# An empty step ahead of the deltas of a selective scan's chunk

## The chip, the cores and the metric

The kernel runs on one core of a Trainium2 chip. The time is device microseconds of one execution of the whole program; the number used is the median of several executions.

## What is computed

The reference takes eight images of 64 x 64 pixels with 96 channels through two layers. Only the first matters here. After a group norm, a projection and a 3 x 3 depthwise convolution, it runs a selective scan (the core of a state-space model) over the 4,096 pixels in four directions `k`, for 192 inner channels with 16 states each:

```python
dts   = einsum('bkrl,kdr->bkdl', x_dbl[:, :, :6], dt_proj_w)
delta = softplus(dts + dt_proj_b)
dA = exp(delta * A)
h  = dA * h + (delta * u) * B
y  = einsum('bkdn,bkn->bkd', h, C)
```

`x_dbl` holds, for each pixel, 6 numbers from which the deltas are made and 16 each of B and C; it is itself a product of the convolved pixels `u` with `x_proj_w`. The four directions are summed, normalised, gated, projected and added to the image. The second layer is a small perceptron on a spectrally upsampled image, filtered and sampled down again.

## The kernel before

**Chunks and tiles.** Each image and direction is cut into 4 chunks of 1,024 pixels, 128 chunks in all. A chunk has 24 tiles: a tile is 8 channels times 16 states on the 128 partitions, with the 1,024 pixels along the free dimension. So there are 3,072 tiles, and the main loop has a step for each. Step numbers below are counted from the chunk's first tile, 0 to 23; tile i is scanned in step i.

**What a tile needs.** TensorE spreads the deltas of 8 channels to 128 partitions with six matmuls into a PSUM tile `pd` (`decay`, L1087), and ScalarE takes the exponential in place (L1095). GpSimd multiplies the fetched delta times u, `dub`, by the broadcast B (`product_b`, L1080). VectorE scans (L1102). The product with C, `hc` (L1108), is made by VectorE for two tiles of three, and by GpSimd for the third (tile number 2 modulo 3), whose scan writes to its own tile `h` and not over `pd`. TensorE adds up the states (`sums`, L1141). `pd` has two buffers, so the decay of tile i + 1 waits until tile i - 1 is done with its buffer: after its scan where GpSimd makes the product, after VectorE's product elsewhere.

**The order of the work.** It is written out by hand; each engine takes its instructions in the order in which the program emits them. Step i issues, in this order: the fetch of tile i + 6 on SyncE's queue, GpSimd's product with C for tile i - 1 if it is GpSimd's, the product with B for tile i + 3, the decay and exponential of tile i + 1, the scan of tile i with VectorE's product and the copy of its last state, then `side.advance`, which lets the side work emit some pieces, and at every second step the sums.

**Side work.** Everything that is not a tile's own is a generator: the convolution, the gates, the perceptron, and `prepare` (L956), which makes what the chunk after needs. Each `yield` states the cost of the piece behind it on each engine and whether it needs one of three PSUM banks. `Side.advance` (L109) adds an allowance to each engine's budget at every step (CAPS, L50) and resumes the running generators, one piece each, if budget and banks allow; a piece marked `more` may follow in the same step, and a piece that doesn't fit waits for the next step. The preparation of a chunk is in the urgent list and goes ahead of the other work, after the stores. `Side.start` (L95) begins a new generator: it fetches the first yield and, if what that asks for is there, runs the first piece in the same step; up to two urgent items can begin in one step.

**The preparation of a chunk**, during the chunk before it. `begin` loads `u`. From step 0 on, `project` (L976) makes the product of `u` with `x_proj_w` in three pieces (L984, bank `px`), and after the third ScalarE copies it with a bias to `xd` (L994). `project` runs alone, so `broadcasts` (B and C to the partitions, by DMA from `xd`, L1005) and `deltas` (L1007) begin in the step in which it ends. `deltas` takes a bank `pv` and, for three groups of 64 channels: the product of `xd` with `dt_w` on TensorE (L1017); absolute value and exponential on ScalarE (L1026, L1027); a piece later logarithm and relu (L1029, L1030), which give softplus; their sum by a matmul with the identity (L1032), copied to `dl` and, as bfloat16, to `dp` (L1035, L1036); then two pieces that subtract what the bfloat16 copy holds and copy the rest (L1041, L1042), with GpSimd's product delta times u (L1040) and the DMAs that write it to memory (L1044). Each group takes five steps. The next group's product comes in the step after the last piece of the group before.

Of the kernel before, what the change touches and what calls it, by code (L numbers as in the profile page):

```python
# [137 lines left out]
def kernel(ctx: ExitStack, tc: tile.TileContext, a: dict, out: bass.AP):  # L138
# [817 lines left out]
    def prepare(b, k, i0, got):  # L956

        v = {}

        def begin():  # L960
            yield {}
            blocks = range(i0 // MB, i0 // MB + 2) if k % 2 else range(8)
            while not all((b, n, blk) in filtered for blk in blocks for n in range(2)):
                yield {}
            assert k % 2 or all((b, n) in laid for n in range(2))
            v["u"] = pp.tile([128, Q3, MB], F32, tag="u", name="u", bufs=1)
            for q in range(Q3):
                yield dict(dma=256)
                for hf in range(2):
                    t0 = i0 + MB * hf  # L970
                    nc.sync.dma_start(
                        v["u"][64 * hf : 64 * hf + 64, q, :], u_dram[b][k % 2][64 * q : 64 * q + 64, t0 : t0 + MB]
                    )
            got["du"] = dr.tile([DI, T], F32, tag="du", name="du")

        def project():  # L976

            xd = v["xd"] = pp.tile([128, MB], F32, tag="xd", name="xd", bufs=1)
            yield dict(bank=1, pe=0.95)
            n, p = side.bank("px")  # L980
            for q in range(Q3):
                for hf in range(2):
                    rows = slice(64 * hf, 64 * hf + 64)
                    nc.tensor.matmul(  # L984
                        p[rows],
                        xp[rows, k, q, :],
                        v["u"][rows, q, :],
                        start=(q == 0),
                        stop=(q == 2),
                        skip_group_check=True,  # L990
                    )
                if q < 2:
                    yield dict(pe=0.95, act=0.7 * q)
            nc.scalar.activation(xd, p, AF.Identity, bias=one)  # L994
            side.give(n)

        def broadcasts():

            xd = v["xd"]
            for name, row in (("br", 48), ("cr", 32)):  # L1000
                t = got[name] = pp.tile([128, T], F32, tag=name, name=name)
                for hf in range(2):
                    yield dict(dma=256)
                    src = xd[64 * hf + row : 64 * hf + row + NS, None, :]
                    nc.sync.dma_start(t[:, MB * hf : MB * hf + MB], src.to_broadcast([NS, 8, MB]))  # L1005

        def deltas():  # L1007

            yield dict(bank=1, pe=0.95, act=1.4)
            n, t = side.bank("pv")  # L1010
            for q in range(Q3):
                if q:
                    yield dict(pe=0.95, act=1.4)
                    t = side.again(n, "pv")
                for hf in range(2):
                    rows = slice(64 * hf, 64 * hf + 64)
                    nc.tensor.matmul(  # L1017
                        t[rows],
                        dt_w[rows, k, 64 * q : 64 * q + 64],
                        v["xd"][rows],  # L1020
                        start=True,
                        stop=True,
                        skip_group_check=True,
                    )
                e = pp.tile([128, MB], F32, tag="e", name="e")
                nc.scalar.activation(e, t, AF.Abs)  # L1026
                nc.scalar.activation(e, e, AF.Exp, scale=-1.0)  # L1027
                yield dict(act=1.4)
                nc.scalar.activation(e, e, AF.Ln, bias=1.0)  # L1029
                nc.scalar.activation(t, t, AF.Relu)  # L1030
                yield dict(pe=0.87, act=1.4)
                nc.tensor.matmul(t, ident, e, start=False, stop=True, skip_group_check=True)  # L1032
                dl = pp.tile([128, MB], F32, tag="e", name="dl")
                dp = got["dp", q] = pp.tile([128, 3, MB], BF16, tag="dp", name="dp", bufs=4)
                nc.scalar.copy(dl, t)  # L1035
                nc.scalar.copy(dp[:, 0, :], t)  # L1036
                for p in range(1, 3):
                    yield dict(pe=0.3, act=0.7, pool=1.3 * (p == 1))
                    if p == 1:
                        nc.gpsimd.tensor_tensor(v["u"][:, q, :], dl, v["u"][:, q, :], ALU.mult)  # L1040
                    nc.tensor.matmul(t, minus, dp[:, p - 1, :], start=False, stop=True, skip_group_check=True)  # L1041
                    nc.scalar.copy(dp[:, p, :], t)  # L1042
                for hf in range(2):
                    nc.sync.dma_start(  # L1044
                        got["du"][64 * q : 64 * q + 64, MB * hf : MB * hf + MB], v["u"][64 * hf : 64 * hf + 64, q, :]
                    )
                got["ready"] = q + 1
            side.give(n)

        return [(1, 0, begin), (1, 0, project), (4, 0, broadcasts), (4, 0, deltas)]  # L1050

    tiles = []
# [314 lines left out]
```

## Time and profile before

| | |
|---|---|
| median of 3 runs | 10,889.11 us (10,886.95 to 10,890.89) |
| the profiled execution, its own time | 10,889.88 us |
| its span, first to last instruction | 10,888.1 us |
| granted TensorE clock, mean | 0.977 |
| before the first scan | 139.2 us |
| between the starts of the first and the last scan | 10,471.3 us, 3,410 ns a step |
| after the start of the last scan | 277.7 us |
| busy: GpSimd (POOL), VectorE (DVE) | 10,172.5 us, 9,965.6 us |
| busy: TensorE (PE), ScalarE (ACT) | 9,406.6 us, 6,891.4 us |

In the profile's lines an engine is followed by the source line, the operation, the tile written and, after `<-`, those read. "idle before" is time in which that engine stood still ahead of those instructions, and the name behind it is what ended the wait. A line of the waits gives the total in microseconds, how often, and the longest.

### The profile page before, as it was taken

To read this page: it belongs to the slowest core of one execution; us is meant where nothing else is said; L and a number is where in the kernel's file an instruction comes from. 1 tells how busy PE (TensorE), PEld (TensorE's weight loads), DVE (VectorE), ACT (ScalarE), POOL (GpSimd) and SP (SyncE) were. 2 spreads that over 40 slices of the span, in tenths; PEclk is the share of its full clock that TensorE was granted. 3 is DMA by queue.
4 is the path that set the end of the run, shared out by engine and by line. 5 is a ranking of instruction groups with operands and counts; after the bars stand their busy time and mean duration, and the time that the engine had idled before them with its cause. 6 is when DMAs were issued, how large, how long until landed. Compare 5 with 4: busy or idle time off the path is not lost. (4 is left out here: it accounts for less than half of the span.)

```text
span 10888.1 us, 152912 instructions
## 1 busy us (share of the span) xinstructions
PE 9406.6 (86%) x52498; PEld 3129.1 (29%) x52498; DVE 9965.6 (92%) x7319; ACT 6891.4 (63%) x10138; POOL 10172.5 (93%) x4674
## 2 busy tenths in 40 slices
PE   7788778988789988899889997898978989789888
PEld 2222222422233222332223322233222432223325
DVE  5999999999999999999999999999999999999990
ACT  5666556767567665666656666566756767566653
POOL 4999999999999999999999999999999999999990
PEclk8999999999999999999999999999999999999998
DMA  6879898898988989898998989899898898988981
GB/s 155 224 200 234 218 236 216 221 235 232 239 214 225 235 233 233 214 225 232 240 228 220 230 223 247 217 225 234 231 237 218 222 232 234 239 214 223 230 207 49
DMA packets 1052725, 2402.30 MB, mean 221 GB/s; under 512 B 302012, under 2 KB 322748, under 8 KB 1051944
## 3 DMA queue, kind: packets, MB, share of 16 engines
q1 hardware_dynamic: 1050968, 2391.48, 87.0%
q8 instruction: 413, 6.77, 0.3%
q14 instruction: 368, 3.01, 0.1%
q10 hardware_dynamic: 976, 1.04, 0.0%
HBM read 1929.05 MB, written 328.73 MB: 207 GB/s over the span
## 5 line engine op out<-in xcount | busy, mean ns | idle before, releaser
L1080 POOL TENSOR_TENSOR bb<-dub,br 128x1024 f32<-128x1024 f32 x3072 | 7183.5, 2367 | 149.2 <-DMA dub<-du 95.6
L1095 ACT ACTIVATE pd<-pd,neg_a 128x1024 f32<-128x1024 f32 x3072 | 3339.4, 1087 | 3051.3 <-PE pd L1087 3026.1
L1102 DVE TENSOR_TENSOR_SCAN pd<-pd,carry,bb 128x1024 f32<-128x1024 f32 x1536 | 3605.4, 2347 | 279.3 <-ACT pd L1095 162.6
L1087 PE MATMUL pd<-dp,sel_b 64*128 64x512 bf16 x18432 | 2596.7, 385 | 1075.4 <-DVE carry L1122 686.6
L1108 DVE TENSOR_TENSOR hc<-pd,cr 128x1024 f32<-128x1024 f32 x2048 | 2508.7, 1225 | 144.8 <-PE py L1141 3.2
L1108 POOL TENSOR_TENSOR hc<-h,cr 128x1024 f32<-128x1024 f32 x1024 | 2423.0, 2366 | 180.3 <-DVE h L1102 151.4
L1102 DVE TENSOR_TENSOR_SCAN h<-pd,carry,bb 128x1024 f32<-128x1024 f32 x768 | 1797.5, 2341 | 1.7 <-ACT pd L1095 1.6
L1141 PE MATMUL py<-hc,sel_r 128*32 128x512 f32 x12288 | 1736.0, 620 | 48.6 <-POOL hc L1108 47.1
L1087 PEld LDWEIGHTS <-sel_b 64*128 64x128 bf16 x18432 | 722.7, 94 | 3602.7 <-issue 1557.1
L1102 DVE TENSOR_TENSOR_SCAN pd<-pd,bb 128x1024 f32<-128x1024 f32 x512 | 1173.3, 2292 | 128.2 <-ACT carry L1122 52.2
L565 PE MATMUL pc<-pad,convr 96*128 96x512 f32 (+1 forms) x2304 | 844.0, 610 | 2.1 <-issue 2.1
L1115 PE MATMUL idle<-xp,ident 128*128 128x384 f32 x1450 | 662.9, 540 | 3.2 <-ACT t1s L807 3.2
L1102 DVE TENSOR_TENSOR_SCAN h<-pd,bb 128x1024 f32<-128x1024 f32 x256 | 583.7, 2280 | 14.8 <-ACT pd L1095 11.6
L1040 POOL TENSOR_TENSOR u<-dl,u 128x512 f32<-128x512 f32 x384 | 491.7, 1280 | 108.7 <-ACT dl L1035 108.7
L1017 PE MATMUL pv<-xd,dt_w 64*64 64x512 f32 x1536 | 425.4, 632 | 166.9 <-ACT xd L994 164.5
L1141 PEld LDWEIGHTS py<-hc,sel_r 128*32 128x32 f32 x12288 | 253.4, 109 | 977.2 <-issue 751.4
L859 PEld LDWEIGHTS p<-w2q,mq 128*100 128x100 f32 x4800 | 461.9, 168 | 169.3 <-issue 135.2
L852 PE MATMUL ph<-xu,w 96*128 96x500 f32 x960 | 493.6, 617 | 16.0 <-ACT xu L846 9.2
L859 PE MATMUL p<-w2q,mq 128*100 128x96 f32 x4800 | 504.2, 256 | 2.3 <-ACT mq L853 2.3
L1032 PE MATMUL pv<-e,ident 128*128 128x512 f32 x768 | 437.1, 651 | 27.9 <-ACT pv L1030 27.0
L1042 ACT CAST dp<-pv 128x512 bf16<-128x512 f32 x768 | 452.1, 589 | 5.0 <-PE pv L1041 5.0
L984 PE MATMUL px<-u,xp 64*64 64x512 f32 x1536 | 417.2, 618 | 5.1 <-DMA u<-u 3.2
(162 smaller groups left out, 8195.4 us busy)
## 6 DMA issues: line engine op xcount, KB each, us to landing
dub<-du SPq DMA_DIRECT2D x3072, 512.0 KB
u<-u SPq DMA_DIRECT2D x768, 128.0 KB
du<-u SPq DMA_DIRECT2D x768, 128.0 KB
y<-yq SPq DMA_DIRECT2D x768, 128.0 KB
br<-xd SPq DMA_DIRECT2D x256, 256.0 KB
cr<-xd SPq DMA_DIRECT2D x256, 256.0 KB
yp<-y SPq DMA_DIRECT2D x384, 128.0 KB
yp<-u SPq DMA_DIRECT2D x192, 128.0 KB
```

Source lines behind the costliest of these rows:

```text
L565: nc.tensor.matmul(t[rows].rearrange("p (i j) -> p i j", i=8), weights[:, cs], v["pad"][:, 8 * blk + kw : 8 * blk + kw + 8, kh : kh + H], ...
L852: nc.tensor.matmul(t[:, :px], w1[:, m, :], xu, start=True, stop=True)
L859: nc.tensor.matmul(t[:SIDE, C * i : C * i + C], sq[:, m, row], w2q[:, m, :], start=(m == 0), stop=(m == 2))
L1040: nc.gpsimd.tensor_tensor(v["u"][:, q, :], dl, v["u"][:, q, :], ALU.mult)
L1042: nc.scalar.copy(dp[:, p, :], t)
L1080: nc.gpsimd.tensor_tensor(t["bb"], t["dub"], t["got"]["br"], ALU.mult)
L1087: nc.tensor.matmul(pd[:, MB * hf : MB * hf + MB], sel_b[rows, 4 * t["s"] + t["j"]].rearrange("p n c -> p (n c)"), t["got"]["dp", t["q"]][r ...
L1095: nc.scalar.activation(pd, pd, AF.Exp, scale=neg_a[:, t["k"], t["g"] : t["g"] + 1])
L1102: nc.vector.tensor_tensor_scan(t["h"][:, ::step], pd[:, ::step], t["bb"][:, ::step], 0.0 if t["first"] else held, ALU.mult, ALU.add)
L1108: (nc.gpsimd if t["by_pool"] else nc.vector).tensor_tensor(t["hc"], t["h"], t["got"]["cr"], ALU.mult)
L1115: nc.tensor.matmul(p, ident, xp[:, 0:2].rearrange("p k q r -> p (k q r)"), start=True, stop=True)
L1141: nc.tensor.matmul(py[r0 : r0 + 32], sel_r[:, t["j"], :], t["hc"][:, MB * hf : MB * hf + MB], start=(t["j"] == 0), stop=(t["j"] == 3 and t ...
```

## The change

One empty step is put at the head of the deltas' generator. An empty `yield {}` needs no budget and no bank: when `deltas` is begun, it runs up to the next yield, and what stands there, the first product of `xd` with `dt_w`, comes in a later step. Everything behind it in the generator moves along.

```diff
         def deltas():
 
+            yield {}
             yield dict(bank=1, pe=0.95, act=1.4)
             n, t = side.bank("pv")
             for q in range(Q3):
```

Lines from L1009 on stand one lower in the changed kernel.

## The prediction

> **What bounds the kernel now.** I read the page first: shares of the engines, then the costliest groups.
>
> ```profile
> PE 9406.6 (86%) x52498; PEld 3129.1 (29%) x52498; DVE 9965.6 (92%) x7319; ACT 6891.4 (63%) x10138; POOL 10172.5 (93%) x4674
> L1080 POOL TENSOR_TENSOR bb<-dub,br 128x1024 f32<-128x1024 f32 x3072 | 7183.5, 2367 | 149.2 <-DMA dub<-du 95.6
> L1102 DVE TENSOR_TENSOR_SCAN pd<-pd,carry,bb 128x1024 f32<-128x1024 f32 x1536 | 3605.4, 2347 | 279.3 <-ACT pd L1095 162.6
> ```
>
> POOL and DVE are both nearly full: three steps hold three scans and two products on DVE (3 x 2.35 + 2 x 1.23 = 9.5 us) and four products of 2.37 us on POOL (9.5 us). From the second to the second-last chunk POOL stands idle for 306 us, DVE for 536 us. No more than this idle time can be won, and only where DVE's wait makes POOL wait too. The waits say what ends them:
>
> ```profile
> DVE pd L1102 <- ACT pd L1095: 202.8, 246, 2.8
> ...
> PE pv L1017 <- ACT xd L994: 164.5, 107, 2.8
> ...
> ACT e L1026 <- PE pv L1017: 139.1, 113, 2.1
> ```
>
> Second line: in 107 places PE stands still at the first product of the deltas, because ScalarE has not copied `xd` yet. Third: ScalarE then waits for that product. First: DVE waits for exponentials. The timeline of one such place, steps 2 to 4 of the 36th chunk, ties the three together (start, duration, engine, line; idle before in brackets):
>
> ```profile
> 3003.37 0.82 PE L1087 MATMUL pd<-dp,sel_b 64*128 64x512 bf16 x6
> ...
> 3004.12 1.07 PE L984 MATMUL px<-u,xp 64*64 64x512 f32 x4
> ...
> 3004.23 1.09 ACT L1095 ACTIVATE pd<-pd,neg_a 128x1024 f32<-128x1024 f32 x1 [2.73 <-PE pd L1087]
> 3005.24 0.59 ACT L1174 COPY yq<-py 128x512 f32<-128x512 f32 x1
> ...
> 3005.72 0.70 ACT L994 ACTIVATE xd<-px,one 128x512 f32<-128x512 f32 x1
> ...
> 3006.47 1.08 PE L1017 MATMUL pv<-xd,dt_w 64*64 64x512 f32 x4 [1.27 <-ACT xd L994]
> ...
> 3007.48 0.82 PE L1087 MATMUL pd<-dp,sel_b 64*128 64x512 bf16 x6
> 3007.59 0.60 ACT L1026 ACTIVATE e<-pv 128x512 f32<-128x512 f32 x1 [1.17 <-PE pv L1017]
> ...
> 3008.22 0.63 ACT L1027 ACTIVATE e<-e 128x512 f32<-128x512 f32 x1
> ...
> 3008.76 1.07 ACT L1095 ACTIVATE pd<-pd,neg_a 128x1024 f32<-128x1024 f32 x1
> ...
> 3009.93 2.36 DVE L1102 TENSOR_TENSOR_SCAN pd<-pd,carry,bb 128x1024 f32<-128x1024 f32 x1 [0.89 <-ACT pd L1095]
> ```
>
> One step holds a chain over two engines: px, xd, pv, absolute value, exponential. Tile 4's decay and exponential are queued behind it, and scan 4 starts 0.89 us late.
>
> **How much room a step has.** Set the end of scan 2 at 0; the decay of tile 4 can start then. Scan 3 with its product ends at 3.6. An exponential starts 0.86 us after its decay's start and takes 1.09, so that of tile 4 must start by 2.5. That of tile 3 ends at about 0 (its decay could start when scan 2 did). ScalarE's side work of step 2 has thus some 2.5 us. It holds the copy of `yq` 0.59, `xd` 0.70, the wait 1.17, 0.60 and 0.63: 3.7, so 1.2 too much, against 0.89 measured here. In the same way the side work of a step 0 modulo 3 has some 3.8 us before a scan is late, and that of 1 modulo 3 some 2.5.
>
> **How often.** I laid the trace against the program's order. The first product stands in the same step as `xd` in 106 chunks: step 2 in 98, step 3 in 7, step 7 in the first. In those 98 DVE's idle time between the starts of scans 3 and 4 is 107.2 us, 1.09 each; in the other 30 chunks, where the product comes a step later (no bank was free) or both fall elsewhere, it is 0.05. The 7 lose 0.95 more than the others, a step later. The trace thus holds its own comparison.
>
> **The change, part by part.** The counts are from the program order of both kernels.
>
> *What goes.* After the change no chunk has `xd` and the first product in one step; 97 chunks have them in steps 2 and 3, 16 in 3 and 4, 14 in later pairs. 98 x (1.09 - 0.05) = 102 us, and 7 x 0.95 = 7. Sum 109.
>
> *What is late next.* Step 2 keeps `yq` and `xd` on ScalarE, 1.3 us of 2.5. Step 3 gets the product and 1.23 us of ScalarE work, of 3.8; the product runs while ScalarE is in tile 4's exponential.
>
> *What moves.* All five pieces of each group come a step later, so the products of the three groups go from residues 2, 1, 0 modulo 3 to 0, 2, 1. From the second chunk on, residues 0, 1, 2 hold 126, 132 and 120 of them after and 126 each before, with the wait for `xd` in 98 of residue 2 and 7 of residue 0. 28 products at residue 2 without the wait are in the trace: DVE's idle time in the step that follows is 0.17 each, no more than the 0.24 of all such steps. So the 92 more cost nothing by this row; if not, see the second rival. GpSimd's delta times u (1.28 us) keeps its count at about the same residues. The 768 DMAs that write it pass one more fetch of `dub` on SP's queue; the first is issued in step 7 and read from step 18 on, 11 steps or 37 us later, so this is covered. The broadcasts stay in the step of `xd`. The chunk's last pieces end at about step 18 instead of 17 of 24.
>
> *What is added.* Eight matmuls that keep TensorE busy in empty steps (725 to 733, each two rows of 0.54 us in the trace), 9 us in steps with almost nothing else on PE. All other work is the same by count. Ahead of the first scan the order changes too: ScalarE and the convolution in front of the first group's identity matmul keep the group's end near 112 us by the rows there; I take 0, within 2 either way. The work behind the last scan is the same.
>
> *What POOL takes back.* In 29 of the 98 chunks POOL's idle time is below the stall; together these stalls are 28 us. POOL runs ahead: its product ends in the median 5.3 us before the scan that reads it, at the least in those chunks 1.1 to 2.9, in three of them 0.3 to 0.8. That lead lets DVE gain one or two stalls before POOL ends last. Bounds 0 and 28; I take 12, nearer to 0, as most such chunks stand singly or in pairs.
>
> *The remaining idle time.* Only 602 of 3,064 steps keep the same list of side matmuls, so the 536 - 114 = 422 us of other idle time on DVE is dealt anew. I take 5 against the change, within 25 either way (6% of it, an estimate).
>
> Sum: -102 - 7 + 12 + 5 = -92. On the profiled execution, 10,889.9 - 92 = 10,798; the median of the runs lies 0.8 below that execution: **10,797**.
>
> **Two rules of the skill.** POOL has the highest share, 93% against DVE's 92%. The Trainium skill, Perfetto Trace Analysis, section Identifying the Most-Contended Engine, says to improve the engine with the highest occupancy first; this change takes nothing from POOL, and read strictly the rule leaves the first rival's time instead of the sum. Its section Optimization Strategy adds that a gap that repeats on the engine that should be full can mean too few buffers; the gap here repeats in 98 chunks and is 0.05 us in 30 with the same buffers, so the trace puts it to order, and by the rule the change would leave all 107 us in place.
>
> **Rivals.** *POOL sets the pace.* For: 97% of the window from 5,000 to 7,000 us:
>
> ```profile
> 5000.00:7000.00 2000.00, 1747.90 (x9576) 549.78 (x9576) 1895.47 (x1386) 1298.00 (x1899) 1936.92 (x888) 0.98 0.91 229
> ```
>
> The third pair is DVE, the fifth POOL. Of a whole 16-chunk image some chunks show no idle POOL at all, and there a chunk with the stall (76.9 us) is no longer than its neighbours without (78.0). Then only POOL's waits for DVE in steps 3 and 4 go: 22.4 for `h` and 21.5 for a `bb` buffer, 44 us, 10,846. Against: POOL idles 101 us in steps 2 to 5 of the 98 chunks.
>
> *The second product becomes the stall.* It goes to a residue-2 step in 92 more chunks, with 2.5 us of room, and tile exponentials are queued behind it. If nothing of it is hidden, each costs the wait 1.23 (139.1 / 113), 0.60 and 0.63: 92 x 2.46 = 226, less 97 won: +129, 11,019, slower. It decides from 97 / 92 = 1.05 us a piece. Against: 0.17 in the 28 of the trace.
>
> *Nothing to measure.* The first product is not delayed where it stalled, or other idle time takes the place of the stalls: within 20 us of 10,889. The program order rules out the first half; the second needs the dealt-anew 422 us to grow by a fifth.
>
> **Chances.** 0.2%, 22 us, is about what a measurement can tell. Forecast case (gain 65 to 139): 0.68. POOL's pace (22 to 65): 0.17. Nothing: 0.08. Second product: 0.07. Faster 0.85, same 0.08, slower 0.07. The range runs from all stalls gone, nothing taken back, and 25 of luck (109 + 5 + 25 = 139, 10,750) to POOL's pace with 19 of bad luck (10,865); the last two cases lie outside.
>
> **What would show it.** After: the wait of L1018 for `xd` is gone from PE, that of L1027 for `pv` is small; DVE's wait for exponentials falls by about half; its idle time between scans 3 and 4 is near 0.05 us a chunk. If POOL's pace holds, DVE waits for `bb` instead. If the second rival holds, DVE's idle time shows after step 8. If the stalls go and the time stays, the first step of the sum that failed is the lead of POOL.

## The result and the profile after

Over 20 runs of each kernel the changed kernel takes 10,912.08 us (10,880.12 to 10,922.65) and the kernel before 10,888.72 us (10,872.58 to 10,906.69). The ratio is 1.0018 with a 95% interval of 1.0012 to 1.0025: about 20 us slower, where 92 us faster was forecast. That is about the 0.2% which the prediction took for what a measurement can tell, and with this many runs it can be told from none. The profiled execution took 10,921.47 us, 9 above the median.

The page's head and two of its groups (busy time and mean ns of one, then idle time before them and what ended most of it):

```profile
span 10919.6 us, 153008 instructions
...
PE 9538.8 (87%) x52514; PEld 3139.6 (29%) x52514; DVE 9966.3 (91%) x7319; ACT 6883.9 (63%) x10138; POOL 10175.3 (93%) x4674
...
L1081 POOL TENSOR_TENSOR bb<-dub,br 128x1024 f32<-128x1024 f32 x3072 | 7205.8, 2381 | 223.7 <-DMA dub<-du 191.0
L1103 DVE TENSOR_TENSOR_SCAN pd<-pd,carry,bb 128x1024 f32<-128x1024 f32 x1536 | 3605.1, 2347 | 302.8 <-ACT pd L1096 166.8
```

The busy times of DVE, ACT and POOL are those of before within 8 us. PE's 132 us more come with only 16 more matmuls, so each lasts a little longer; the granted clock, 0.972 against 0.977, would make some 48 of them (an estimate, 0.5% of 9,407). The clock does not sort the kernels below: two_step_project has 0.972 too and is faster than the kernel before, early_all has 0.977 and is slower. As PE is not full, the time is to be sought in idle time. GpSimd's idle time ahead of the product with B has grown from 149 to 224 us, and what ends it is the fetch of `dub`: 95.6 before, 191.0 now. The waits (total, times, longest) of the changed kernel, and behind them three lines of the kernel before:

```profile
PEld py L1142 <- POOL hc L1109: 227.9, 133, 4.7
DVE pd L1103 <- ACT pd L1096: 205.3, 242, 5.7
POOL bb L1081 <- DMA dub<-du: 191.0, 148, 5.8
...
DVE pd L1103 <- ACT carry L1123: 142.9, 161, 5.6
...
PE py L1142 <- POOL hc L1109: 121.1, 78, 3.8
```

```profile
PEld py L1141 <- POOL hc L1108: 100.2, 71, 4.5
...
POOL bb L1080 <- DMA dub<-du: 95.6, 86, 6.1
...
PE py L1141 <- POOL hc L1108: 47.1, 46, 3.5
```

Two waits that stood here before are gone from this list: that of the first product for `xd` (164.5) and that of ScalarE for the product (139.1). The first and the last line of the changed kernel have grown: TensorE's sums (PE), and their weight loads (PEld), wait for GpSimd's product with C, 227.9 and 121.1 us where it was 100.2 and 47.1. DVE's wait for exponentials (second line) was to fall by half and is where it was (202.8).

I sorted DVE's idle time in the scan loop by the step it falls in. It went from 548 to 570 us. Step 3, where the stall was, went from 109 to 9 us; all other steps together went from 440 to 562. Most of that is in steps 2 (51 to 88), 14 (31 to 84) and 20 (38 to 62). So the loop lost 22 us; before the first scan it is 143.1 us instead of 139.2, and after the start of the last 282.5 instead of 277.7. Together that is the difference of some 31 us between the two profiled executions.

The timeline of the changed kernel around one such place, steps 13 to 15 of the 34th chunk (start, duration, engine, line; idle before in brackets):

```profile
2850.01 2.35 POOL L1081 TENSOR_TENSOR bb<-dub,br 128x1024 f32<-128x1024 f32 x1 [1.09 <-DMA dub<-du]
...
2852.31 1.27 POOL L1041 TENSOR_TENSOR u<-dl,u 128x512 f32<-128x512 f32 x1
...
2853.54 2.34 POOL L1109 TENSOR_TENSOR hc<-h,cr 128x1024 f32<-128x1024 f32 x1
...
2854.61 2.34 DVE L1103 TENSOR_TENSOR_SCAN h<-pd,carry,bb 128x1024 f32<-128x1024 f32 x1
...
2855.94 1.36 PE L1142 MATMUL py<-hc,sel_r 128*32 128x512 f32 x4 [1.97 <-POOL hc L1109]
...
2857.23 1.46 PE L1088 MATMUL pd<-dp,sel_b 64*128 64x512 bf16 x6
...
2858.73 1.09 ACT L1096 ACTIVATE pd<-pd,neg_a 128x1024 f32<-128x1024 f32 x1 [4.38 <-PE pd L1088]
...
2859.92 2.36 DVE L1103 TENSOR_TENSOR_SCAN pd<-pd,carry,bb 128x1024 f32<-128x1024 f32 x1 [2.97 <-ACT pd L1096]
```

Read it downwards. A late fetch holds GpSimd for 1.09 us. GpSimd then does delta times u, which stands right ahead of `hc` of tile 11, so this `hc` ends at 2855.88. The sums of tiles 10 and 11 wait 1.97 us for it on TensorE. Queued behind them is the decay of tile 15, then its exponential, and scan 15 starts 2.97 us late. The fetch is not all of it: without its 1.09 us some 1.9 of the 2.97 would be left (an estimate, their difference), as GpSimd was behind already. Its product with B for tile 12 had ended 0.77 us ahead of scan 12, where 5.3 is the median of the kernel before. In the changed kernel, some 60 of the 70 us of long stalls (over 0.5 us) in step 14 come with such a wait of the sums; before it was 10 of 26. In the whole trace the weight loads of the sums waited for a product of GpSimd 185 times for 179 us before, and 259 times for 328 us after.

The theory, called the fetch theory below: the change removes the stall, but with the other side work dealt to other steps by the budgets of `Side.advance` (called re-dealt from here on), fetches of `dub` come late; GpSimd loses its lead, and its late `hc` comes back to DVE through the sums on TensorE. Rivals: it is where delta times u now stands in GpSimd's queue; it is the new place of the deltas' later pieces; the stall of step 3 was worth nothing.

The expectations below name theories by letters. A is the new place of what moved: of delta times u in runs 1 to 4 and 10, of all moved work in run 5, of the deltas' later pieces in runs 8 and 9. B is GpSimd's pace with the fetches, and C the other work dealt anew.

### The profile page after: what moved, and what is told of

It reads as the page before. It is cut to its first block, busy times and chain, and to the rows that moved or that the text cites. A ratio compares the mean times of both kernels' runs of the same rounds, so it can differ in the third digit from the quotient of the medians.

```text
span 10919.6 us, 153008 instructions
## 1 busy us (share of the span) xinstructions
PE 9538.8 (87%) x52514; PEld 3139.6 (29%) x52514; DVE 9966.3 (91%) x7319; ACT 6883.9 (63%) x10138; POOL 10175.3 (93%) x4674
## 5 line engine op out<-in xcount | busy, mean ns | idle before, releaser
L1081 POOL TENSOR_TENSOR bb<-dub,br 128x1024 f32<-128x1024 f32 x3072 | 7205.8, 2381 | 223.7 <-DMA dub<-du 191.0
L1096 ACT ACTIVATE pd<-pd,neg_a 128x1024 f32<-128x1024 f32 x3072 | 3339.5, 1087 | 3231.9 <-PE pd L1088 3211.7
L1142 PE MATMUL py<-hc,sel_r 128*32 128x512 f32 x12288 | 1817.8, 624 | 121.6 <-POOL hc L1109 121.1
```

Of the source, the lines that this page charges most:

```text
L1081: nc.gpsimd.tensor_tensor(t["bb"], t["dub"], t["got"]["br"], ALU.mult)
L1096: nc.scalar.activation(pd, pd, AF.Exp, scale=neg_a[:, t["k"], t["g"] : t["g"] + 1])
L1142: nc.tensor.matmul(py[r0 : r0 + 32], sel_r[:, t["j"], :], t["hc"][:, MB * hf : MB * hf + MB], start=(t["j"] == 0), stop=(t["j"] == 3 and t ...
```

## The experiments

Ratios are against the kernel before, run beside each kernel on the same chip, with a 95% interval.

**1. Delta times u one piece earlier (u_early).** The changed kernel, with GpSimd's product back at about its old steps.

```diff
-                yield dict(pe=0.87, act=1.4)
+                yield dict(pe=0.87, act=1.4, pool=1.3)
...
                 nc.scalar.copy(dp[:, 0, :], t)
+                nc.gpsimd.tensor_tensor(v["u"][:, q, :], dl, v["u"][:, q, :], ALU.mult)
                 for p in range(1, 3):
-                    yield dict(pe=0.3, act=0.7, pool=1.3 * (p == 1))
-                    if p == 1:
-                        nc.gpsimd.tensor_tensor(v["u"][:, q, :], dl, v["u"][:, q, :], ALU.mult)
+                    yield dict(pe=0.3, act=0.7)
```

> The changed kernel with GpSimd's product delta times u issued one piece earlier, in the piece that makes dl, so that it stands at steps 5, 10 and 15 as before the change and not at 6, 11 and 16; the first product stays a step behind xd. Theory A (the place of that product): at step 11 it stands right ahead of GpSimd's product with C for tile 11, TensorE's sums wait for that one, the decay of tile 15 is queued behind the sums; so VectorE's idle time of step 14 falls from 84 us to the 31 us of before, and the median from 10,912 to about 10,850. Theory B (GpSimd and the fetches set the pace, wherever that product stands): idle time moves to other steps, the median stays at 10,912 within 15.

Measured: 10,921.32 us, ratio 1.0029 [1.0018, 1.0041], as B had it. The idle time of step 14 fell to 38 us, but steps 2, 8 and 5 had 99, 40 and 32, GpSimd waited 77 us more for `dl`, and still 179 us for fetches. In this pair the place of the product decides in which step the loss shows, not how much is lost.

**2. Delta times u one piece later, in the kernel before (u_late_before).**

```diff
-                    yield dict(pe=0.3, act=0.7, pool=1.3 * (p == 1))
-                    if p == 1:
+                    yield dict(pe=0.3, act=0.7, pool=1.3 * (p == 2))
+                    if p == 2:
```

> The kernel before with only GpSimd's product delta times u put a piece later, to steps 6, 11 and 16 as in the changed kernel; the first product stays in the step of xd. Theory A: the stall after xd stays (VectorE idle about 109 us in step 3) and step 14 gains some 50 us of idle time, 10,940. Theory B: 10,889 within 15, since GpSimd does the same work.

Measured: 11,063.16 us, 1.0160 [1.0146, 1.0174], slower than either theory said. Without any change to the first product, GpSimd's waits for fetches went to 213.5 us, step 2 to 138 us and DVE's idle time to 718. The cost entry moves too, which deals the other work anew; run 10 takes the two apart.

**3. The other way to part `xd` and the product (two_step_project).** The changed kernel, with the third piece of `project` in the step of the second, so that `xd` comes in step 1 and the product in step 2.

```diff
-                    yield dict(pe=0.95, act=0.7 * q)
+                    yield dict(pe=0.95 * (1 - q), act=0.7 * q, more=bool(q))
```

> The changed kernel with the projection's second and third piece in one step, so that xd is made in step 1 and the first product and all behind it stand at steps 2 to 17, nearly as before the change; only the wait for xd is gone. Theory A: no product is moved to a bad place, the 100 us of step 3 are won, about 10,800. Theory B: VectorE's idle time of step 3 goes and comes back elsewhere, with the sums waiting for GpSimd and GpSimd for the fetches: 10,880 within 25.

Measured: 10,864.01 us, 0.9975 [0.9965, 0.9986]. Step 3 is down to 10 us of idle time, but step 2 is up to 135: two products `px` now stand ahead of the decay of tile 3. The later pieces are at their old steps, and fetch waits are 121 us. The time is within B's bounds. The stall moved by a step, and yet this order is faster than both kernels.

**4. The sums a step later (sums_late).** The changed kernel, to take the sums out from between GpSimd's `hc` and the decay.

```diff
-            ends = i % 2 == 1 and 3 <= i <= n + 2
+            ends = i % 2 == 0 and 4 <= i <= n + 3
...
-                sums(tiles[i - 3 : i - 1])
+                sums(tiles[i - 4 : i - 2])
```

> The changed kernel with the sums of each pair of tiles issued one step later on TensorE, behind one more decay. Both theories: the sums' wait for GpSimd no longer holds up the decay of the tile that is due next, so VectorE's idle time of steps 2, 14 and 20 falls from 234 us to about 120, and sums still wait without harm. Theory A: 10,810. Theory B: VectorE then waits for bb instead, 10,880 within 25. A third theory, that the order of the side work was only dealt badly: no direction is given, idle time in other steps.

Measured: 11,741.03 us, 1.0793 [1.0774, 1.0813]. A miss, and one that tells nothing of the theories: `hc` has four buffers, and with the sums a step later both engines that write it wait for a free one, as the waits of this kernel show:

```profile
DVE hc L1109 <- PE py L1142: 1226.7, 900, 4.9
...
POOL hc L1109 <- PE py L1142: 671.8, 337, 5.9
```

**5. Only the first product later (defer_first).** The kernel before, with all its yields and costs. The first group's product, Abs and Exp are issued at the head of the next piece, with Ln and Relu, and no other instruction changes its step.

```diff
+                if not q:
+                    yield dict(act=1.4)
                 for hf in range(2):
...
                 nc.scalar.activation(e, e, AF.Exp, scale=-1.0)
-                yield dict(act=1.4)
+                if q:
+                    yield dict(act=1.4)
```

> The kernel before with its budget and steps untouched, but the first group's product, absolute value and exponential issued at the head of the next piece, together with the logarithm and the relu. So in the same 106 chunks the wait for xd is gone, and not one other instruction changes its step: the side work is not dealt anew, delta times u and its DMAs stay. If what took the gain back is the new place of the other work (theory A in its wide form: every piece behind the first moved, and the planner dealt the rest anew), the gain is kept: VectorE's idle time of step 3 falls from 109 us to about 10, 10,800. If GpSimd's pace and the fetches take it back wherever the work stands (theory B), the idle time returns as waits for GpSimd's products and for the fetched deltas: 10,870 or more.

Measured: 10,808.22 us, 0.9934 [0.9921, 0.9946], near what A had, 75 us faster than the 10,883.47 beside it. This is the best full kernel of the study; it beats both. It is also the test of the last rival: 104 us less idle time in step 3 were worth 75 us of time. Step 3 has 5 us left, and the waits read:

```profile
PEld py L1144 <- POOL hc L1111: 150.4, 123, 4.7
...
DVE pd L1105 <- ACT pd L1098: 117.4, 175, 4.3
POOL bb L1083 <- DMA dub<-du: 114.1, 110, 6.1
```

Here the wait for exponentials falls by 42% (202.8 to 117.4), as the prediction wanted, and fetch waits go from 96 to 114 us only. The sums wait more here too (150 us where it was 100), so a part of that comes with the gain itself.

**6 and 7. Half the fetches (half_dub_before, half_dub_after).** In both kernels an odd tile uses the fetched `dub` of its even neighbour.

```diff
     def fetch(t):
+        if t["i"] % 2:
+            t["dub"] = pair[0]["dub"]
+            return
+        pair[:] = [t]
         t["dub"] = sp.tile([128, T], F32, tag="dub", name="dub", bufs=4)
```

> The kernel before with half of the fetches of the deltas times u left out: an odd tile multiplies with what its even neighbour fetched, so the products are other numbers. The 1,536 fetches and 786 MB less leave room on the DMA queue. GpSimd's 90 us of waits for the fetch should be near 0; some 10,830 if that is worth 60 us. It is the ground for the next kernel.

> The same with the changed kernel. If the fetches took the gain back (GpSimd's waits for them rose from 90 to 185 us), this kernel is faster than the halved kernel before by most of the 100 us of step 3: ratio of the two about 0.992. If they were only where a GpSimd that is late anyway happened to wait, the two stay within 0.3% of each other.

Measured: 10,822.24 us, 0.9948 [0.9934, 0.9961], and 10,756.35 us, 0.9882 [0.9867, 0.9898]. With half the fetches the change is worth -66 us (0.61%); with all of them it costs about 20. In the changed kernel step 14 falls from 84 to 25 us. Its windows view (PE, PEld, DVE, ACT, POOL busy, then granted clock, DMA share and GB/s) and its waits:

```profile
5000.00:7000.00 2000.00, 1759.57 (x9717) 552.38 (x9717) 1920.61 (x1416) 1309.81 (x1923) 1960.84 (x900) 0.98 0.64 155
```

```profile
DVE pd L1108 <- ACT pd L1101: 124.5, 220, 2.6
...
PEld py L1147 <- POOL hc L1114: 93.9, 66, 4.5
```

The DMA share falls from 0.92 (this window in the changed kernel) to 0.64, the fetch wait to 9.5 us, and the weight loads of the sums wait 94 us instead of 228. This supports the fetch theory. It doesn't tell late issue from a loaded DMA, since the four buffers also last for eight tiles here.

**8 and 9. Place and dealing, one at a time (early_all, defer_all).** The change does two things: it puts the deltas' later pieces a step later, and it moves their cost entries, so that the other work is dealt anew. early_all has the changed kernel's dealing, with the later pieces back in their old steps; defer_all has the dealing of before, with all pieces a step later. The diffs show the end of each generator alone.

```diff
+            w = work()
             yield {}
+            for at, cost in enumerate(costs):
+                yield cost
+                next(w, None)
+                if not at:
+                    next(w)
```

```diff
+            for at, cost in enumerate(costs):
+                yield cost
+                if at:
+                    next(w)
+                else:
+                    held = side.bank("pv")
+            yield {}
+            next(w)
+            next(w, None)
```

(`work` is the body of `deltas` with bare yields, `costs` the list of its fifteen costs.)

> All other work in every step exactly as in the changed kernel; the deltas' own instructions a step earlier than there, except the first product, which stays behind xd (the logarithm and relu join it). So this is the deltas' place of the deferred kernel that took 10,808 us, with the order that the planner dealt in the changed kernel. If the dealing of the other work took the gain back (theory C), it is as slow as the changed kernel, 10,910 within 20. If the new place of the deltas' later pieces took it back (theory A), it is near 10,810.

> The opposite corner: every piece of the deltas a step later, as in the changed kernel, with budgets and yields as before, so that the other work keeps its step but for the bank that is held a step longer. Theory C: about 10,815, as the deferred kernel. Theory A: about 10,910, with VectorE's idle time of step 14 near 84 us.

Measured: early_all 10,911.48 us, 1.0034 [1.0023, 1.0045]; defer_all 10,879.59 us, 1.0004 [0.9995, 1.0012]. Beside defer_first (0.9934), either one alone costs 0.7 to 1.0%, and both together (the changed kernel, 1.0018) cost 0.8%: the two do not add up. The kernel of the old places and the new dealing came where C had it; the other came between the two theories. So the new place of the deltas' later pieces is not needed for the loss (early_all), and it costs something by itself (defer_all).

**10. Only the product, not its cost entry (u_late_place).** The kernel before, with delta times u a step later, and nothing else moved.

```diff
                     yield dict(pe=0.3, act=0.7, pool=1.3 * (p == 1))
-                    if p == 1:
+                    if p == 2:
```

> The kernel before with GpSimd's delta times u a step later and its budget entry left where it was, so that no other instruction changes its step; the earlier kernel with that product a step later had moved the budget too and took 11,063 us. Theory A: slow again, above 11,000. Theory C: the product's place costs little, 10,890 within 25, and the 173 us of the earlier kernel came from the work that was dealt anew.

Measured: 10,973.18 us, 1.0090 [1.0076, 1.0104], 99 us slower than the kernel beside it. From its waits, GpSimd's for the fetch and that of SyncE's own queue for delta times u:

```profile
POOL bb L1080 <- DMA dub<-du: 162.9, 144, 6.1
```

```profile
SPq L1044 <- POOL u L1040: 1086.6, 378, 9.2
```

SyncE's wait in the kernel before, then in the changed one:

```profile
SPq L1044 <- POOL u L1040: 107.3, 151, 9.2
```

```profile
SPq L1045 <- POOL u L1041: 178.6, 249, 9.2
```

The write of `u` is now issued in the step of the product itself, so SyncE's queue stands still for it in 378 places and not in 151 (107.3 us before), with the next fetches of `dub` behind it. The mean time from a buffer coming free to its fetch being issued grew from 0.82 to 1.25 us. This goes with a loss about as large as the stall itself; both theories missed it. The changed kernel has some of that wait too, 249 places and 178.6 us, but its mean time to the issue of a fetch is the 0.82 us of before. This run also bears on the place in GpSimd's queue: delta times u stands right ahead of `hc` of tile 11 in 92 chunks here and in 98 of the changed kernel, and step 14 has 34 us of idle time here, 84 there. The place alone does not make that stall.

**11 and 12. Without delta times u on GpSimd (no_u_before, no_u_after).**

```diff
-                    if p == 1:
-                        nc.gpsimd.tensor_tensor(v["u"][:, q, :], dl, v["u"][:, q, :], ALU.mult)
```

> The kernel before without GpSimd's product delta times u: u itself is written and fetched, so the scans run on other numbers. GpSimd has 384 x 1.28 = 492 us less to do and is no longer full. The ground for the next kernel; some 10,800 if VectorE's own work and its stalls then bound it.

> The same with the changed kernel. If the gain was taken back because GpSimd is full and each late fetch moves all that follows, a GpSimd with room makes it up, and the gain is kept: ratio of the two about 0.993. If the late fetches or the dealing of TensorE's and ScalarE's work take it back without GpSimd, the two stay within 0.2% of each other.

Measured: 10,832.09 us, 0.9954 [0.9942, 0.9967], and 10,809.17 us, 0.9935 [0.9921, 0.9949]. The intervals overlap, so in time this pair is inconclusive. The product with B in the two profiles, the second of which is of that kernel's fastest run (10,773 us):

```profile
L1078 POOL TENSOR_TENSOR bb<-dub,br 128x1024 f32<-128x1024 f32 x3072 | 7167.9, 2357 | 352.4 <-DMA dub<-du 266.2
```

```profile
L1079 POOL TENSOR_TENSOR bb<-dub,br 128x1024 f32<-128x1024 f32 x3072 | 7174.3, 2361 | 430.0 <-DMA dub<-du 368.4
```

In each, some 105 us are one wait ahead of the loop; in the loop GpSimd idles for fetches 160 and 265 us, so part of the relief went into waiting. These kernels have no delta times u on GpSimd, and SyncE has nothing of GpSimd's to wait for ahead of that write. The fetch waits still rise by 105 us from the old order to the new. So neither the place of that product nor SyncE's wait for it is needed to make fetches late.

**13 to 15. The other three orders with half the fetches (half_defer_first, half_early_all, half_defer_all).** The edits of runs 5, 8 and 9 on top of that of run 6. They ask whether the loss of run 7 and that of runs 8 and 9 go the same way.

> The deferred kernel (only the wait for xd taken away) with half of the fetches left out, as in the other halved kernels. The gain of the deferral should stay what it was with all fetches, 0.9934: so 0.9948 x 0.993 = 0.988 of the kernel before. It is the ground for the next two.

> The other work as the changed kernel deals it, the deltas' later pieces in their old steps, half of the fetches left out. With all fetches the dealing cost 1.0% against the deferred kernel. If that went through late fetches, it shrinks to 0.3% or less here; if it is TensorE's and ScalarE's own order, it stays near 1%.

> The deltas' later pieces a step later, the other work nearly as before, half of the fetches left out. With all fetches the place cost 0.7% against the deferred kernel. If through late fetches, 0.3% or less here; if through the third group's chain in a step without room on TensorE and ScalarE, it stays near 0.7%.

Measured: 10,731.31 us, 0.9866 [0.9849, 0.9882]; 10,803.30 us, 0.9929 [0.9914, 0.9944]; 10,799.20 us, 0.9926 [0.9911, 0.9940]. All ten side by side, with DVE's idle time in the loop by step (us, one profiled execution each):

| fetches | order | ratio | idle, all | step 2 | 3 | 5 | 14 | 20 | others |
|---|---|---|---|---|---|---|---|---|---|
| all | before | 1 | 548 | 51 | 109 | 19 | 31 | 38 | 300 |
| all | defer_first | 0.9934 | 469 | 60 | 5 | 25 | 42 | 40 | 297 |
| all | early_all | 1.0034 | 566 | 79 | 9 | 70 | 31 | 35 | 342 |
| all | defer_all | 1.0004 | 545 | 91 | 5 | 11 | 88 | 30 | 320 |
| all | changed | 1.0018 | 570 | 88 | 9 | 25 | 84 | 62 | 302 |
| half | before | 0.9948 | 481 | 28 | 103 | 21 | 22 | 36 | 271 |
| half | defer_first | 0.9866 | 399 | 33 | 5 | 25 | 15 | 49 | 272 |
| half | early_all | 0.9929 | 460 | 27 | 7 | 70 | 16 | 25 | 315 |
| half | defer_all | 0.9926 | 456 | 38 | 5 | 9 | 67 | 24 | 313 |
| half | changed | 0.9882 | 419 | 30 | 8 | 20 | 25 | 48 | 288 |

With all fetches the changed order has 101 us more idle time than defer_first, and 92 of them are in steps 2, 14 and 20 (28 + 42 + 22). With half the fetches it has 20 us more, and 6 of them in these three. In time the distance shrinks from 0.85% (1.0018 / 0.9934) to 0.16% (0.9882 / 0.9866). So some four fifths of that distance go with the fetches (0.69 of 0.85), which is as much as the stall itself was worth (0.66).

For early_all and defer_all the fetch theory fails: with half the fetches they still are 0.64% and 0.61% behind defer_first, where 0.3% or less was expected if it held, with stalls of their own (step 5 in the one, step 14 in the other) that fetches do not cure. What these two have in common is that the cost entries no longer stand in the steps where the pieces are. That this mismatch makes the stalls was only argued; no run tests it.

## Why the prediction was wrong, point by point

**What bounds the kernel; the chain of step 3.** Right. `px`, `xd`, product, Abs and Exp in one step hold the next tile's exponential. Deferring the product took step 3 from 109 to 5 us in defer_first and to 9 in the changed kernel.

**"98 x (1.09 - 0.05) = 102 us, and 7 x 0.95 = 7."** Right for the stall; alone it gave 75 us in time (defer_first). The other 34 of the 109 are what GpSimd takes back (predicted 12, between 0 and 28) and what else moved: other idle time grew from 440 to 464 us in defer_first.

**"What is late next"** (step 3 holds the product in 3.8 us of room). Right: 9 us.

**"So the 92 more cost nothing by this row."** The row was 28 products that already stood at residue 2, with an idle time of 0.17 us each in the step that follows. The second rival, with DVE idle after step 8, didn't come: steps 8 and 9 went from 21 and 8 to 20 and 18 us. But pieces were not compared where their neighbours change. Of delta times u the text said that it keeps "its count at about the same residues"; it went from a place ahead of `hc` of tile 5 to one ahead of `hc` of tile 11, in 98 chunks each. With all fetches step 14 has 84 us of idle time in that order, with half of them 25.

**"What POOL takes back ... I take 12."** The mechanism was right, the size too small. The median lead of its product over the scan went from 5.3 to 4.6 us in defer_first, where fetches held it little longer than before: that is DVE gaining on GpSimd. In the changed kernel the median is 4.5, hardly less. What differs is the low end: the smallest lead of a chunk, median over the chunks, is 2.7 us before, 1.8 in defer_first and 1.0 in the changed kernel, in which fetches held GpSimd 191 us in place of 96. GpSimd is not the bound by its own work either; in the loop it idled for 335 us against 317.

**"Ahead of the first scan ... I take 0, within 2 either way. The work behind the last scan is the same."** 3.9 and 4.8 us more in the profiled executions, one of each kernel.

**"The remaining idle time ... I take 5 against the change, within 25 either way."** This is the step that failed. The text had the right number beside it: only 602 of 3,064 steps keep their side matmuls. It then called the re-dealt 422 us a matter of luck of 6%. Measured over the whole loop, the idle time outside step 3 grew by 122 us, 28%, in place of 5; that is more than the 100 us that step 3 gave. Against defer_first, 92 of the 101 us of difference stand in steps 2, 14 and 20, and 6 with half the fetches: so the greater part of what the term left out goes with the fetches of `dub`. The last rival, "Nothing to measure", named this mechanism ("the dealt-anew 422 us to grow by a fifth") and was given 0.08; it is what came, and a little more. The 6% had no row behind it, and two rows pointed the other way: the DMA share of 0.91, and GpSimd's 95.6 us for late fetches, in the loop the largest item of its idle time after the 151.4 us of waiting for scans.

**SP's queue: "pass one more fetch of `dub` on SP's queue ... so this is covered."** True for the fetches that read what is written. Not asked was what stands behind the writes: SyncE waits for `u` in 249 places instead of 151, and the fetches queue behind it; but runs 11 and 12 have late fetches without that wait. In the changed kernel 148 fetches instead of 86 are late enough to hold GpSimd, and those are issued 3.4 us instead of 2.8 after their buffer came free. In SyncE's order a load of `yp` stands right ahead of 41 of them instead of 28, one of the perceptron (`t1r`, `t3r`) ahead of 31 instead of 7; that these loads are what delays them is not shown.

**The signs named.** PE's wait for `xd` gone: yes. DVE idle near 0.05 us a chunk between scans 3 and 4: 8.5 / 128 = 0.07, yes. DVE's wait for exponentials down by half: no, 202.8 to 205.3, for the late decays of steps 2, 14 and 20 took the place. "The first step of the sum that failed is the lead of POOL": only in so far as the lead shrank, which it did in defer_first too, with the gain kept.

**The two rules weighed.** The Trainium skill, Perfetto Trace Analysis, section Identifying the Most-Contended Engine, would have had GpSimd relieved first. Leaving out its product delta times u (three a chunk at 1.28 us, 3 x 128 x 1.28 = 491 us of GpSimd's time) gave 0.46% in the kernel before, less than deferring one product on TensorE gave (0.66%). The section Optimization Strategy says that a repeated gap can mean too few buffers; here deferring the product took the gap from 109 to 5 us with all buffers as they were.

**What stays open.** Which of the transfers dealt anew make the fetches late, and whether by their place in the queue or by the load on the DMA. The traces lean to the queue: from its issue to the product that waits for it, a late fetch takes 8.8 us before and 8.7 after on average, while its issue went from 2.8 to 3.4 us behind the free buffer. But these are the late ones alone. An earlier fetch with more buffers of `dub` would tell; it wasn't tried. And place and dealing can't be parted cleanly, since the two kernels that part them have stalls of their own.

## What to carry to other kernels

When a change moves one instruction in a hand-made schedule, ask what other work the budgets deal anew by it, and price that at its own size. Here deferring the one product without touching the cost entries gave 0.66%, where the empty step lost 0.18%. Where three resources are nearly full at once (here GpSimd 97%, VectorE 95% and the DMA 0.91 in mid-run), removing an idle time of one need not shorten the whole: 100 us less in step 3 gave 75 us or cost 20, by what became of the fetches. So look at the waits of the feeding transfer first. A comparison inside a trace, stalled places against others, holds for the stall and says nothing of the rest of the schedule.

## What was not expected of the hardware

A GpSimd product of 1.28 us that moves by one step in its queue, with nothing added, cost 99 us over the run (u_late_place), more than the 75 that removing the stall is worth; with it SyncE's wait for that product went from 107 to 1,087 us and GpSimd's for fetches from 96 to 163. A late fetch reaches the scan through four engines (GpSimd's `hc`, sums on TensorE, exponential on ScalarE, scan on VectorE); in the place shown the scan came 2.97 us late. And halving the fetches, with a DMA share of 0.92 down to 0.64, gave only 0.5% to the kernel before but 1.4% to the changed one (0.9882 / 1.0018): the same transfers cost more or less by the order in which the other work stands around them.
